# A four-layer graph network on one core: gate columns as products of their own, and a last layer with five whole blocks, paired normalisations and an early overflow count

## The chip, the cores and the metric

The kernel runs on one core of one Trainium2 chip. A core has a matrix engine (TensorE, PE in the profile, with its weight loads as PEld), a vector engine (VectorE, DVE), an activation engine (ScalarE, ACT), a general engine that here mostly issues gathers (GpSimd, POOL), a queue engine (SyncE, SP) and 16 DMA engines. The metric is the device time of one execution in microseconds (us), as the median of several executions. One profiled execution gives the trace that is read below.

## The reference, cut to what matters

There are 2708 nodes with 512 features each. The adjacency matrix is sparse and sorted so that its first rows and columns are the densest. Four layers follow each other, each with a residual and a layer normalisation.

```python
x = layernorm(x + L0(x, adj))          # normalised adjacency @ x @ W.T + b
x = layernorm(x + L1(x, adj))          # (adj + scaled mask) @ x, over its row sums
# layer 2: attention and plain convolution, each with a gate
attn_a = sigmoid(concat([adj @ x, x]) @ Wa.T + ba)
attn_b = sigmoid(concat([adj @ x, x]) @ Wb.T + bb)
h   = x @ W_sa
x_a = softmax_like(adj, h) @ h
x_b = adj @ (x @ W_gcnb) + b_gcnb
x = layernorm(x + sigmoid(attn_a * x_a + attn_b * x_b))
# layer 3
xw = (x > 0) @ sign(weight).T
x = layernorm(x + relu(adj @ xw))
```

## The kernel before

The 2708 nodes make 22 blocks of 128 rows (the last has 20). For every block of rows the kernel finds at its start which columns of the adjacency are not zero, and keeps the columns' numbers (`index`) and their values, packed into tiles of 128 columns (`packed`). Block b has room for `ROOM[b]` such tiles; should one have more, a counter `n_over` is above zero and a dense version of all layers runs afterwards, in an `If` at the end. With these inputs it doesn't run. In a layer, each tile of a block is a gather of 128 rows of features by an indirect DMA, issued by GpSimd, and a matmul.

```python
ROOM = (0, 9, 8, 7, 7, 6, 6, 6, 5, 5, 5, 5, 5, 4, 4, 4, 4, 4, 4, 4, 4, 1)


DIRECT = {1: (0, 1), 2: (0,), 3: (0,), 5: (0,), 8: (0,), 9: (0,),
          13: (0,), 14: (0,), 15: (0,), 16: (0,), 17: (0,)}
...
WHOLE3 = 4
```

The overflow counter is made at the end of the search, as a float:

```python
        nc.tensor.matmul(tot[0:1, :NB], ones, found, start=True, stop=True)
        n_over = const.tile([1, 1], F32, name="s_n_over")
        nc.vector.tensor_tensor(room, tot[0:1, :NB], room, op=ALU.is_gt)
        nc.vector.tensor_reduce(n_over, room, axis=AX.X, op=ALU.add)
```

In layer 2 a block accumulates adj @ x and the attention sums, transposed, in `acc`; they are copied to `pt` and multiplied by the weights. The two columns by which the gates weigh adj @ x lie beside the 512 columns of `W_gcnb`, so that the second half of that product is 258 wide and goes, with the attention's sum, into the PSUM tile `pc`:

```python
        H = D // 2

        def project2(b: int):
            m = rows(b)
            st = state[b]
            acc = st["acc"]
            pt = op.tile([P, KC, 2, P], F32, tag="pt", name=f"pt2_{b}", bufs=1)
            for k in range(0, KC, 2):
                nc.scalar.copy(
                    pt[:, k : k + 2, :, :m],
                    acc[:, k : k + 2, :].rearrange("p k (h i) -> p k h i", h=2)[:, :, :, :m],
                )
            pc = ps_s2.tile([P, KC * P], F32, tag="sm", name=f"pc{b}")
            nc.tensor.matmul(pc[:m, 0:1], st["esum"][:, :m], ones, start=True, stop=True)
            ph = ps_pr.tile([P, D], F32, tag="pr", name=f"ph{b}")
            pg = ps_pr.tile([P, D], F32, tag="pr", name=f"pg{b}")
            for h, ps, w in (
                (0, pg[:m, :H], wg[:, :, :H]), (0, pc[:m, 1 : H + 3], wg[:, :, H:]),
                (1, ph[:m], wsa),
            ):
                for k in range(KC):
                    nc.tensor.matmul(
                        ps, pt[:, k, h, :m], w[:, k, :], start=(k == 0), stop=(k == KC - 1)
                    )
            st.update(pc=pc, ph=ph, pg=pg)

        def finish2(b: int):
            ...
            t = work.tile([P, D], F32, tag="t", name=f"t2_{b}")
            nc.vector.tensor_scalar(t[:m], bg_row[:m], att[:m, 1:2], None, op0=ALU.mult)
            for th, ps in ((t[:m, :H], pg[:m, :H]), (t[:m, H:], pc[:m, 1 : H + 1])):
                nc.vector.scalar_tensor_tensor(
                    th, ps, att[:m, 1:2], th, op0=ALU.mult, op1=ALU.add
                )
            nc.vector.scalar_tensor_tensor(
                t[:m], ph[:m], att[:m, 3:4], t[:m], op0=ALU.mult, op1=ALU.add
            )
```

The last layer splits every adjacency value into a high and a low part, so a tile takes two matmuls (`halves_of`: one copy on ScalarE, one subtraction on VectorE), and widens the features from 16 bits (`widened`). The first `WHOLE3` = 4 blocks take all columns, with no gather: their adjacency comes as a 128 x 512 tile per column block (`whole_tile`), and their four sums stay in PSUM. The others gather. Six whole tiles go ahead, then two after each gathered block:

```python
    with tc.tile_pool(name="s_l3", bufs=13, reuse_waits="tile") as lp, \
            tc.tile_pool(name="s_ps_w", bufs=1, reuse_waits="tile", space=PSUM) as ps_w, \
            tc.tile_pool(name="s_ps_3", bufs=4, reuse_waits="tile", space=PSUM) as ps_3:
...
        def finish3(b: int, ps):
            m = rows(b)
            old = f[b] if b else first[1]
            t = work.tile([P, D], F32, tag="t", name=f"t3_{b}")
            nc.vector.scalar_tensor_tensor(
                t[:m], ps[:m], 0.0, old[:m, :D], op0=ALU.max, op1=ALU.add
            )
            o = work.tile([P, D], F32, tag="xb", name=f"o{b}")
            last = layernorm(o[:m], t, m, f"3_{b}")
            nc.sync.dma_start(out[b * P : b * P + m, :], o[:m])
            return last

        sources3 = {}

        def gather3(b: int):
            sources3[b] = [gathered(lp, D, xw_rows, b, t, F32R) for t in range(ROOM[b])]

        gather3(WHOLE3)


        whole = [ps_w.tile([P, D], F32, tag=f"w{b}", name=f"l3_{b}") for b in range(WHOLE3)]


        def whole_tile(j: int):
            ...
            a = lp.tile([P, W3], F32, tag="aw", name=f"aw{j}", bufs=4)
            nc.sync.dma_start(a[:r], adj_t[j * P : j * P + r, :W3])
            p = halves_of(a[:r], r, W3, f"w{j}")
            for b in range(WHOLE3):
                for h in range(2):
                    nc.tensor.matmul(
                        whole[b], p[:r, h, b * P : (b + 1) * P], g[:r, :],
                        start=(j == 0 and h == 0), stop=(j == NB - 1 and h == 1),
                    )
            if j == NB - 1:
                for b in range(WHOLE3):
                    finish3(b, whole[b])

        AHEAD3 = 6
        for j in range(AHEAD3):
            whole_tile(j)
        j = AHEAD3
        for b in range(WHOLE3, NB):
            ...
            xo = widened(xo, m, f"o{b}")
            if b > WHOLE3:
                gather3(b)
            src = [xw0] * len(direct(b)) + sources3.pop(b)
            ...
            for h in range(2):
                nc.tensor.matmul(
                    ps[:m], dp[:m, h, :m], xo[:m, :], start=(h == 0), stop=False
                )
            ...
                for i in range(n):
                    for h in range(2):
                        nc.tensor.matmul(
                            ps[:m], p[:, h, i * m : (i + 1) * m], src[i0 + i],
                            start=False, stop=(i0 + i == len(src) - 1 and h == 1),
                        )
            last = finish3(b, ps)
            for _ in range(2):
                if j < NB:
                    whole_tile(j)
                    j += 1
        with tc.issue_after(last.ins):
            nc.vector.tensor_copy(over, n_over)
```

`layernorm` there is nine small or wide operations: `bn_stats` and `bn_aggr` on VectorE, a square root on ScalarE with one Newton step on VectorE, and the scaling of the row on VectorE. The outer kernel ends with the test of the counter:

```python
    n_over = nc.values_load(over[0:1, 0:1], min_val=0, max_val=-(-x.shape[0] // P))
    with tc.If(n_over > 0):
        dense_layers(tc, *args)
```

## Time and profile before

| what | value |
|---|---|
| time, median of 3 | 1090.33 us (1087.86 to 1091.51) |
| span of the profiled execution | 1088.5 us |
| PE busy | 956.7 us, 88% |
| DVE busy | 729.7 us, 67% |
| POOL busy | 535.7 us, 49% |
| ACT busy | 404.2 us, 37% |
| bytes moved by DMA | 193.53 MB, mean 178 GB/s |

How it is read: a busy share is an average over stages that have different limits, so it says little by itself. The view of busy time by stage, the waits of one engine, the chain of work that ended last and the groups by line of the kernel say what ends a stage. A matrix multiplication in 32-bit floats appears as two instructions. PEld runs beside PE. A tensor's name in the profile is that of the program with the buffer number left out: `pc`, `pg`, `ph` are products of layer 2, `px` its last product, `pw` and `p` the split tiles, `xg` a gathered tile, `l` a sum of the last layer, `t` and `o` the rows before and after normalisation.

### The profile page before, as it was taken

The numbers are of one execution on the slowest core, as the hardware profiler recorded it, in microseconds if no ns is written. First come the engines' busy times: TensorE is split into PE (matmuls) and PEld (weight loads), VectorE is DVE, ScalarE is ACT, GpSimd is POOL, SyncE is SP. The second block draws the span as 40 slices with busy tenths as digits, with TensorE's granted clock in tenths as the row PEclk, the third lists the DMA queues.
The fourth block names the chain that finished last, engine by engine and source line by source line (L and its number), as shares of the span: only waits on it lengthen the run. The fifth ranks groups of instructions, "written<-read, shape, count | busy, mean of one in ns | idle before, by whom it ended". The sixth has DMA issues, their size and how long they took to land. (4 is left out here: it accounts for less than half of the span.)

```text
span 1088.5 us, 13527 instructions
## 1 busy us (share of the span) xinstructions
PE 956.7 (88%) x4009; PEld 607.7 (56%) x4028; DVE 729.7 (67%) x2578; ACT 404.2 (37%) x869; POOL 535.7 (49%) x545
## 2 busy tenths in 40 slices
PE   2999991899996899998999999999999999789972
PEld 1545440344442345556767777777777777577740
DVE  3998895357774878886576665556666564357865
ACT  4666650010001466785233322322323332165520
POOL 0577777777764777752323223312312221067771
PEclk9999995899996999999999999999999999989995
DMA  9999955778875678872323222322311212199993
GB/s 315 333 385 351 322 173 149 231 237 247 246 247 200 203 220 238 237 211 87 99 63 94 78 64 80 86 69 55 97 53 54 79 45 59 58 312 361 300 261 111
DMA packets 84523, 193.53 MB, mean 178 GB/s; under 512 B 13680, under 2 KB 26968, under 8 KB 84440
## 3 DMA queue, kind: packets, MB, share of 16 engines
q0 software_dynamic: 41056, 113.12, 37.1%
q1 hardware_dynamic: 31692, 64.45, 16.9%
q10 hardware_dynamic: 11692, 15.01, 4.2%
q8 instruction: 34, 0.56, 0.2%
q14 instruction: 49, 0.40, 0.1%
HBM read 155.73 MB, written 25.92 MB: 167 GB/s over the span
## 5 line engine op out<-in xcount | busy, mean ns | idle before, releaser
L1494 POOL DMA_INDIRECT xg<-x_rows,i x107 | 104.0, 972 | 210.6 <-DVE mv L619 59.1
L1336 PE MATMUL acc<-ae,xg 128*128 128x256 f32 x856 | 187.6, 378 | 0.0
L1336 PEld LDWEIGHTS acc<-ae,xg 128*128 128x128 f32 x856 | 162.1, 190 | 22.1 <-ACT ae L1329 0.4
L928 POOL DMA_INDIRECT a<-in_adj_t_dram,row_at x107 | 116.9, 1092 | 65.7 <-DVE mask L782 34.0
L570 POOL DMA_INDIRECT xg<-x_rows,i x107 | 112.0, 1047 | 49.0 <-issue 21.0
L1254 PE MATMUL l<-xg,a 128*128 128x512 f32 x214 | 104.9, 626 | 25.8 <-DMA xg<-y_rows,i 25.8
L570 POOL DMA_INDIRECT xg<-y_rows,i x107 | 104.2, 974 | 32.6 <-issue 17.1
L1400 PE MATMUL l<-xg,inc 128*128 128x512 f32 x214 | 101.1, 609 | 11.9 <-DMA xg<-x_rows,i 10.4
L570 POOL DMA_INDIRECT xg<-xw_rows,i x83 | 83.4, 1005 | 32.6 <-issue 11.9
L958 PE MATMUL y<-s_w,xt 128*128 128x512 f32 (+1 forms) x176 | 84.4, 624 | 0.0
L621 POOL TENSOR_TENSOR rs<-mv,s_neg_half 128x1 f32<-128x1 f32 (+1 forms) x22 | 12.7, 577 | 137.9 <-DVE mv L619 137.6
L1254 PEld LDWEIGHTS l<-xg,a 128*128 128x128 f32 x214 | 39.3, 195 | 73.3 <-issue 57.7
L1537 PE MATMUL ph<-s_wsa,pt 128*128 128x512 f32 (+1 forms) x176 | 79.1, 592 | 0.0
L1325 ACT ACTIVATE ae<-sl,xg 128x128 f32<-128x128 f32 x107 | 40.5, 394 | 103.5 <-DMA xg<-x_rows,i 91.3
L1400 PEld LDWEIGHTS l<-xg,inc 128*128 128x128 f32 x214 | 39.6, 192 | 66.9 <-issue 32.4
L1336 PE MATMUL acc<-ae,f 128*128 128x256 f32 (+1 forms) x272 | 66.5, 389 | 5.9 <-ACT ae L1377 2.9
L1326 DVE SCALAR_TENSOR_TENSOR ae<-ae 128x128 f32<-128x128 f32 (+4 forms) x69 | 29.0, 421 | 63.7 <-ACT ae L1325 63.7
L1336 PEld LDWEIGHTS acc<-ae,f 128*128 128x128 f32 (+1 forms) x272 | 52.2, 194 | 23.1 <-issue 8.9
L615 DVE BATCH_NORM_STATS2 st<-t 128x6 f32<-128x512 f32 (+1 forms) x88 | 60.6, 689 | 1.1
L733 ACT ACTIVATE unused<-arow 128x1408 uint8<-128x1408 f32 (+3 forms) x44 | 58.3, 1325 | 1.1 <-DMA arow<-in_adj_dram 0.3
L1740 PE MATMUL l<-xg,p 128*128 128x512 f32 (+1 forms) x166 | 48.9, 419 | 10.4 <-DMA xg<-xw_rows,i 9.9
L599 ACT ACTIVATE rsqs<-mv 128x1 f32<-128x1 f32 (+1 forms) x66 | 13.3, 202 | 117.7 <-DVE mv L619 113.0
(251 smaller groups left out, 1778.8 us busy)
## 6 DMA issues: line engine op xcount, KB each, us to landing
arow<-in_adj_dram SPq DMA_DIRECT2D x21, 704.0 KB
arow<-in_adj_dram SPq DMA_DIRECT2D x21, 650.0 KB
x_rows<-f SPq DMA_DIRECT2D x21, 258.0 KB
aw<-in_adj_t_dram SPq DMA_DIRECT2D x21, 256.0 KB
out_dram<-o SPq DMA_DIRECT2D x21, 256.0 KB
f<-in_x_dram SPq DMA_DIRECT2D x20, 256.0 KB
y_rows<-yt ACTq DMA_DIRECT2D x20, 256.0 KB
x_rows<-f SPq DMA_DIRECT2D x20, 256.0 KB
```

What stands on the lines that cost most here:

```text
L570: nc.gpsimd.indirect_dma_start(out=t[:, :dst_w], out_offset=None, in_=src[:, :], in_offset=bass.IndirectOffsetOnAxis(ap=index[b][:, i : i ...
L615: nc.vector.bn_stats(st[:m], t[:m])
L733: nc.scalar.activation(unused[:m, : ar.shape[1]], ar, AF.Copy, accum_out=row_sums[:m, b, h : h + 1])
L928: nc.gpsimd.indirect_dma_start(out=packed[b][:, t + len(direct(b)), :], out_offset=None, in_=adj_t, in_offset=bass.IndirectOffsetOnAxis(ap ...
L958: nc.tensor.matmul(ps[:m], xt[:, k, :m], w0[:, k, :], start=(k == 0), stop=(k == KC - 1))
L1254: nc.tensor.matmul(ps[:m], packed[b][:, i, :], moving[:, :D], start=(i == 0), stop=(i == len(src) - 1),)
L1325: nc.scalar.activation(ev[:, i, :], sl, AF.Identity, bias=score)
L1336: nc.tensor.matmul(acc[:, k, :].rearrange("p (h i) -> p h i", h=2)[:, :, :m], src[:r, k * P : (k + 1) * P], ae[:r, :, :m], start=(is_first ...
L1400: nc.tensor.matmul(ps[:m], inc[:, i, :m], src[i0 + i][:, :D], start=(i0 + i == 0), stop=(i0 + i == len(src) - 1),)
L1494: nc.gpsimd.indirect_dma_start(out=g, out_offset=None, in_=x2_rows[:, :], in_offset=bass.IndirectOffsetOnAxis(ap=index[b][:, t : t + 1], a ...
L1537: nc.tensor.matmul(ps, pt[:, k, h, :m], w[:, k, :], start=(k == 0), stop=(k == KC - 1))
L1740: nc.tensor.matmul(ps[:m], p[:, h, i * m : (i + 1) * m], src[i0 + i], start=False, stop=(i0 + i == len(src) - 1 and h == 1),)
```

## The change

It has four parts. In layer 2 the gates' two columns get a weight tile of their own (`wab`) and four narrow products per block, and the product with `W_gcnb` is done in one piece of 512 columns, with one VectorE operation after it in place of two. In the last layer five blocks take all columns in place of four; the block of 20 rows is gathered first; whole tiles are handed out by the number of gathers done (one for every three) in place of two a block, with five ahead; and there are 11 gather buffers in place of 13. Normalisations of the last layer are done for two blocks together: their small operations are shared, and ScalarE writes the rows; a whole block is the partner of a gathered one near the end. Finally the overflow counter is copied to its integer already in the search, and not after the last row. The purpose is to take gathers from GpSimd, to spread the end's work on VectorE, and to let the engines test the counter without waiting for the last row.

```diff
--- before.py
+++ after.py
@@ -37,7 +37,11 @@
 GROUPS = (
     (1,), (2, 3), (4, 5, 6), (7, 8, 9), (10, 11, 12), (13, 14, 15), (16, 17, 18), (19, 20), (21,),
 )
-WHOLE3 = 4
+
+
+WHOLE3 = 5
+AHEAD3 = 5
+FETCHES3 = 3
 
 
 def over_partitions(row: bass.AP, n: int):
@@ -1135,9 +1139,10 @@
             nc.vector.memset(room[:, b : b + 1], float(P * ROOM[b]))
         tot = ps_s.tile([P, D], F32, tag="find", name="tot", bufs=2)
         nc.tensor.matmul(tot[0:1, :NB], ones, found, start=True, stop=True)
-        n_over = const.tile([1, 1], F32, name="s_n_over")
+        n_over = pre.tile([1, 1], F32, name="s_n_over")
         nc.vector.tensor_tensor(room, tot[0:1, :NB], room, op=ALU.is_gt)
         nc.vector.tensor_reduce(n_over, room, axis=AX.X, op=ALU.add)
+        nc.vector.tensor_copy(over, n_over)
 
     work = ctx.enter_context(tc.tile_pool(name="s_work", bufs=2, side="right", reuse_waits="tile"))
 
@@ -1284,8 +1289,9 @@
     nc.scalar.dma_start(own_row[:, 1, :], over_partitions(wb[0, D:], D))
     bg_row = wp2.tile([P, D], F32, name="s_bg_row")
     nc.scalar.dma_start(bg_row, over_partitions(b_gcnb, D))
-    wg = wp2.tile([P, KC, D + 2], F32, name="s_wg")
-    nc.scalar.dma_start(wg[:, :, :D], w_gcnb.rearrange("(k p) o -> p k o", p=P))
+    wg = wp2.tile([P, KC, D], F32, name="s_wg")
+    nc.scalar.dma_start(wg, w_gcnb.rearrange("(k p) o -> p k o", p=P))
+    wab = wp2.tile([P, 2, KC], F32, name="s_wab")
     l2_ps = ctx.enter_context(ExitStack())
     ps_acc = l2_ps.enter_context(
         tc.tile_pool(name="s_ps_acc", bufs=2, side="right", reuse_waits="tile", space=PSUM)
@@ -1358,10 +1364,7 @@
     with tc.tile_pool(name="s_l1", bufs=8, reuse_waits="tile") as lp:
         pv = ps_mm.tile([P, D], F32, tag="mm", name="pv2")
         nc.tensor.transpose(pv[:, : 2 * KC], vrows, ident[: 2 * KC, : 2 * KC])
-        nc.vector.tensor_copy(
-            wg[:, :, D:].rearrange("p k t -> p t k"),
-            pv[:, : 2 * KC].rearrange("p (t k) -> p t k", t=2),
-        )
+        nc.vector.tensor_copy(wab.rearrange("p t k -> p (t k)"), pv[:, : 2 * KC])
 
         def grow2(j: int, n: int):
 
@@ -1513,8 +1516,6 @@
                     b, st["src"][i0 + i], ae[:, i], P, c == 0 and i == 0, last and i == n - 1
                 )
 
-        H = D // 2
-
         def project2(b: int):
             m = rows(b)
             st = state[b]
@@ -1527,15 +1528,16 @@
                 )
             pc = ps_s2.tile([P, KC * P], F32, tag="sm", name=f"pc{b}")
             nc.tensor.matmul(pc[:m, 0:1], st["esum"][:, :m], ones, start=True, stop=True)
+            for k in range(KC):
+                nc.tensor.matmul(
+                    pc[:m, 1:3], pt[:, k, 0, :m], wab[:, :, k], start=(k == 0), stop=(k == KC - 1)
+                )
             ph = ps_pr.tile([P, D], F32, tag="pr", name=f"ph{b}")
             pg = ps_pr.tile([P, D], F32, tag="pr", name=f"pg{b}")
-            for h, ps, w in (
-                (0, pg[:m, :H], wg[:, :, :H]), (0, pc[:m, 1 : H + 3], wg[:, :, H:]),
-                (1, ph[:m], wsa),
-            ):
+            for h, ps, w in ((0, pg, wg), (1, ph, wsa)):
                 for k in range(KC):
                     nc.tensor.matmul(
-                        ps, pt[:, k, h, :m], w[:, k, :], start=(k == 0), stop=(k == KC - 1)
+                        ps[:m], pt[:, k, h, :m], w[:, k, :], start=(k == 0), stop=(k == KC - 1)
                     )
             st.update(pc=pc, ph=ph, pg=pg)
 
@@ -1547,7 +1549,7 @@
             att = small.tile([P, 4], F32, tag="att", name=f"att{b}")
             nc.vector.tensor_scalar(att[:m, 2:3], pc[:m, 0:1], SUM_EPS, None, op0=ALU.add)
             nc.vector.reciprocal(att[:m, 2:3], att[:m, 2:3])
-            nc.vector.tensor_tensor(att[:m, 0:2], pc[:m, H + 1 : H + 3], own[:m, 1:3], op=ALU.add)
+            nc.vector.tensor_tensor(att[:m, 0:2], pc[:m, 1:3], own[:m, 1:3], op=ALU.add)
 
 
             nc.scalar.activation(att[:m, 0:2], att[:m, 0:2], AF.Tanh, scale=0.5)
@@ -1557,10 +1559,9 @@
             )
             t = work.tile([P, D], F32, tag="t", name=f"t2_{b}")
             nc.vector.tensor_scalar(t[:m], bg_row[:m], att[:m, 1:2], None, op0=ALU.mult)
-            for th, ps in ((t[:m, :H], pg[:m, :H]), (t[:m, H:], pc[:m, 1 : H + 1])):
-                nc.vector.scalar_tensor_tensor(
-                    th, ps, att[:m, 1:2], th, op0=ALU.mult, op1=ALU.add
-                )
+            nc.vector.scalar_tensor_tensor(
+                t[:m], pg[:m], att[:m, 1:2], t[:m], op0=ALU.mult, op1=ALU.add
+            )
             nc.vector.scalar_tensor_tensor(
                 t[:m], ph[:m], att[:m, 3:4], t[:m], op0=ALU.mult, op1=ALU.add
             )
@@ -1633,9 +1634,9 @@
 
 
 
-    with tc.tile_pool(name="s_l3", bufs=13, reuse_waits="tile") as lp, \
+    with tc.tile_pool(name="s_l3", bufs=11, reuse_waits="tile") as lp, \
             tc.tile_pool(name="s_ps_w", bufs=1, reuse_waits="tile", space=PSUM) as ps_w, \
-            tc.tile_pool(name="s_ps_3", bufs=4, reuse_waits="tile", space=PSUM) as ps_3:
+            tc.tile_pool(name="s_ps_3", bufs=3, reuse_waits="tile", space=PSUM) as ps_3:
         W3 = WHOLE3 * P
         CH3 = 4
         PW = max(CH3 * P, W3)
@@ -1660,24 +1661,48 @@
                 nc.scalar.copy(g[:r], t[:r])
             return g
 
-        def finish3(b: int, ps):
+        moments = []
+
+        def finish3(b: int, ps, more: bool):
+
             m = rows(b)
             old = f[b] if b else first[1]
-            t = work.tile([P, D], F32, tag="t", name=f"t3_{b}")
+            k = len(moments)
+            t = work.tile([P, D], F32, tag=("t", "xb")[k], name=f"t3_{b}")
             nc.vector.scalar_tensor_tensor(
                 t[:m], ps[:m], 0.0, old[:m, :D], op0=ALU.max, op1=ALU.add
             )
-            o = work.tile([P, D], F32, tag="xb", name=f"o{b}")
-            last = layernorm(o[:m], t, m, f"3_{b}")
-            nc.sync.dma_start(out[b * P : b * P + m, :], o[:m])
-            return last
+            st = small.tile([P, 6], F32, tag="st", name=f"st_3_{b}")
+            nc.vector.bn_stats(st[:m], t[:m])
+            mv = moments[0][2] if k else small.tile([P, 2, 2], F32, tag="mv3", name=f"mv_3_{b}")
+            nc.vector.bn_aggr(mv[:m, k, :], st[:m])
+            moments.append((b, t, mv))
+            if more:
+                return
+            n = len(moments)
+            rs = small.tile([P, 2, 2], F32, tag="rs3", name=f"rs_3_{b}")
+            mean, v = mv[:m, :n, 0], mv[:m, :n, 1]
+            nc.vector.tensor_scalar(v, v, LN_EPS, None, op0=ALU.add)
+            rsqrt_of(rs[:m, 0, :n], v, m, n, f"3_{b}")
+            nc.vector.scalar_tensor_tensor(
+                rs[:m, 1, :n], mean, -1.0, rs[:m, 0, :n], op0=ALU.mult, op1=ALU.mult
+            )
+            for k, (b, t, _) in enumerate(moments):
+                nc.scalar.activation(
+                    t[:m], t[:m], AF.Identity, bias=rs[:m, 1, k : k + 1],
+                    scale=rs[:m, 0, k : k + 1],
+                )
+                nc.sync.dma_start(out[b * P : b * P + m, :], t[:m])
+            moments.clear()
 
         sources3 = {}
 
         def gather3(b: int):
             sources3[b] = [gathered(lp, D, xw_rows, b, t, F32R) for t in range(ROOM[b])]
 
-        gather3(WHOLE3)
+        order3 = [NB - 1, *range(WHOLE3, NB - 1)]
+        gather3(order3[0])
+        gather3(order3[1])
 
 
         whole = [ps_w.tile([P, D], F32, tag=f"w{b}", name=f"l3_{b}") for b in range(WHOLE3)]
@@ -1699,21 +1724,18 @@
                         whole[b], p[:r, h, b * P : (b + 1) * P], g[:r, :],
                         start=(j == 0 and h == 0), stop=(j == NB - 1 and h == 1),
                     )
-            if j == NB - 1:
-                for b in range(WHOLE3):
-                    finish3(b, whole[b])
-
-        AHEAD3 = 6
-        for j in range(AHEAD3):
+        j = 0
+        while j < AHEAD3:
             whole_tile(j)
-        j = AHEAD3
-        for b in range(WHOLE3, NB):
+            j += 1
+        due = 0
+        for at, b in enumerate(order3):
             m = rows(b)
             xo = lp.tile([P, D], F16, tag="xo", name=f"xo{b}", bufs=3)
             nc.sync.dma_start(xo[:m], xw_rows[b * P : b * P + m, :])
             xo = widened(xo, m, f"o{b}")
-            if b > WHOLE3:
-                gather3(b)
+            if at + 1 < len(order3) and at:
+                gather3(order3[at + 1])
             src = [xw0] * len(direct(b)) + sources3.pop(b)
             ps = ps_3.tile([P, D], F32, tag="mm", name=f"l3_{b}")
 
@@ -1741,13 +1763,17 @@
                             ps[:m], p[:, h, i * m : (i + 1) * m], src[i0 + i],
                             start=False, stop=(i0 + i == len(src) - 1 and h == 1),
                         )
-            last = finish3(b, ps)
-            for _ in range(2):
-                if j < NB:
-                    whole_tile(j)
-                    j += 1
-        with tc.issue_after(last.ins):
-            nc.vector.tensor_copy(over, n_over)
+            pending = bool(moments)
+            finish3(b, ps, not pending and b not in (order3[0], order3[-1]))
+            if j == NB and whole and len(moments) == 1:
+                finish3(WHOLE3 - len(whole), whole.pop(0), False)
+            due += ROOM[b]
+            while j < NB and due >= FETCHES3:
+                whole_tile(j)
+                j += 1
+                due -= FETCHES3
+        while whole:
+            finish3(WHOLE3 - len(whole), whole.pop(0), len(whole) % 2 == 1)
```

## The prediction, made before the change was run

> **What bounds the kernel now.** I read the page's slices first: TensorE (PE) is busy at 0.9 or more for most of the span, with its clock granted in full, and the last slices sag. Busy time by stage then gives two stages that the change touches. The second stretch below is the first half of the last layer, the third and fourth its thin end (columns: window, length, busy us and count of PE, PEld, DVE, ACT, POOL, granted clock, DMA share, GB/s):
>
> ```profile
> 500.00:955.00 455.00, 432.51 (x1870) 327.34 (x1888) 269.69 (x815) 139.71 (x362) 116.70 (x129) 0.99 0.26 72
> 955.00:1026.00 71.00, 69.28 (x291) 55.43 (x292) 52.39 (x131) 38.85 (x81) 53.76 (x53) 0.97 1.15 335
> 1026.00:1059.00 33.00, 25.04 (x85) 15.13 (x84) 24.08 (x87) 11.52 (x31) 25.06 (x27) 0.95 0.98 278
> 1059.00:1088.50 29.50, 7.79 (x22) 2.93 (x20) 16.45 (x66) 1.53 (x8) 4.57 (x5) 0.61 0.39 120
> ```
>
> Layer 2 (500 to 955) is TensorE's: 432.5 of 455 us. What PE waits for there, from 560 to 955, is little, and no gather is among it:
>
> ```profile
> PE pc L1537 <- ACT pt L1524: 9.8, 16, 0.9
> PE tb L1582 <- DVE bx L1574: 5.1, 1, 5.1
> PE px L1587 <- ACT xt L1584: 1.0, 2, 0.7
> ```
>
> So every us of work added to TensorE in layer 2 is a us of span. The last layer is different. The chain that ended last shows whole tiles (L1698) and block products (L1740) without a break at first, then gathers, then a VectorE tail:
>
> ```profile
> 1015.17 3.63 PE l L1698 x16
> 1019.25 2.27 PE l L1740 x10
> ...
> 1052.44 4.20 DMA xg<-xw_rows,i
> 1056.69 1.22 PE l L1740 x2
> ...
> 1072.32 0.68 DVE t L1667
> 1073.13 0.60 DVE st L615
> ```
>
> The group of the gathers says why: 83 of them, 0.94 us each, from 956.4 to 1063.8, a start every (1063.85 - 956.38)/82 = 1.31 us. GpSimd issues them without a pause in 108 us while PE needs only 394 matmuls x 0.227 us (3.63 us for 16) = 89 us, and 1.8 us more because the first eight run cold (628 ns each, starting 0.45 us apart). The last matmul ends near 1069.8; four whole blocks finished at once have left VectorE behind, so the last row is issued at 1075.85, 119.8 us after the layer's first matmul (956.08). Then 12.65 us pass with no work. The lines of the closing code show it:
>
> ```profile
> L1783 POOLq TENSOR_LOAD <-over x1: 492/492/492, 1075.9 to 1075.9; - x1
> L1784 POOLq COMPARE_BRANCH  x1: 53/53/53, 1076.5 to 1076.5; - x1
> L1824 POOLq DRAIN  x3: 50/107/7173, 1080.5 to 1088.2; - x3
> SPq L1824 <- PEq L1824: 6.3, 2, 5.7
> ```
>
> All engines load the overflow count only after VectorE copied it, at 1075.9; GpSimd branches, starts its drain at 1080.5 and holds everybody for 7.17 us. SyncE is ready at 1082.1 and waits 5.7 us.
>
> **What the Trainium skill says.** "TensorE: Matmul & The Clock Gate", section LDWEIGHTS: a load costs its columns divided by 1.2 in ns, 107 for 128 columns. The trace agrees where the moving operand is short: eight f32 matmuls of 40 columns in layer 2 follow each other every 0.111 us, each with its own load. The same page, section on the HAM clock gate, has a cold array for about 3.4 us; here the first eight matmuls of the layer take 3.58 us. "DMA: Bandwidth & Descriptors", section "Where 436 GB/s comes from", has an HBM limit near 358 GB/s per core; this trace moves 356 to 380 in the windows from 960 to 1010, so the last layer's transfers are near a limit as well. "Runtime: NRT & Kernel Launch", section on instruction fetch, has a taken branch fetch its target; here an engine does nothing for 3.3 to 3.9 us after the branch.
>
> **The change, part by part.** *Layer 2, the gate columns.* Before, the two columns rode on the second half of the W_gcnb product (258 instead of 256 columns). An f32 matmul is two instructions, so a block had 8 of 256 columns at 0.2155 and 8 of 258 at 0.2175 us: 3.46 us. After, 8 of 512 columns at 0.4295 = 3.44 us (the spacing of the same shape in `ph`), plus 4 matmuls of 2 columns = 8 instructions that cost their weight loads, 8 x 0.111 = 0.89 us. Net +0.86 us for each of 21 blocks, and about 0.6 for the block of 20 rows: **+18.7 us**, all on the path. VectorE gets one 512-column operation (0.75 as for `ph`) in place of two of 0.48, and the gates' numbers come 3.4 us earlier; neither sets PE's pace, so I count nothing for them.
>
> *Last layer, five whole blocks.* Block 4's seven gathers go: 76 remain. PE gets 22 x 5 x 2 = 220 whole-tile matmuls, 76 x 2 + 8 x 2 block products and 17 x 2 for the blocks' own rows: 422 x 0.227 = 95.8, with the cold start 97.6 us. GpSimd: 75 x 1.31 + 0.3 = 98.6 us to the last gather's start, and 2.8 us to its landing (1063.85 to 1066.66 in the trace) = 101.4. The two are now almost equal, which is what the interleaving is for: a whole tile (10 matmuls, 2.27 us) for every three gathers (3.9 us). Up to block 14, 52 gathers and 17 tiles after the first five, PE has 356 matmuls = 80.8 + 1.8 us; the eleven gather buffers let GpSimd be 11 gathers ahead, so 13 are left, 13 x 1.31 + 2.8 = 19.8 us. That sums to 102.4 us for the last matmul, without any slip. DMA has about the bytes of before: 76 x 262 KB of gathers, 22 x 459 KB of tiles, 2.2 MB of own rows and 5.5 MB out = 37.7 MB, of which 1.8 MB come early; at 365 GB/s 98 us. Three limits within 5 us will not mesh without loss: I add 1.5 us.
>
> *Normalisation in pairs.* VectorE per block before: 0.68 + 0.69 + 0.18 + 0.15 + 0.15 + 0.21 + 0.14 + 0.15 + 0.54 = 2.9 us. A pair after: twice (0.68 + 0.69 + 0.18), once about 1.04 of small ones: 2.07 per block. Some 17 us leave VectorE, and ScalarE gets 22 x 0.63, in a layer where it is busy 38.85 of 71 us. On the path only the end counts: the backlog of 6.0 us between the last matmul and the last issue becomes one block's chain: 0.68 + 0.69 + 0.18 + 0.15, the root 0.20 and two handovers of 0.1, 0.15 + 0.21 + 0.14 + 0.15 + 0.15, 0.63 on ScalarE: 3.5, with a little still queued 4.1 us. First matmul to last issue: 102.4 + 1.5 + 4.1 = 108 instead of 119.8: **-11.8 us**.
>
> *Overflow count.* GpSimd can load it after its last gather, at 99.5 us of the layer; 4.6 us to its drain and 7.2 in it (the durations above) make 111.3. SyncE reaches its own end 6.3 us after the last issue (1075.85 to 1082.12), at 114.3. The drain is hidden: **-5.6 us**.
>
> Sum: 1090.3 + 18.7 - 11.8 - 5.6 = 1091.6, say 1092 us.
>
> **Rivals.** (a) The small matmuls are nearly free because PE idles for `pt` anyway (9.8 us in 16 waits, which stand exactly there). Against it: they need `pt` too, so they come after the wait. If half were hidden: 1083. (b) The reverse: before, the two wide `pc` matmuls (0.87 us) covered the 0.6 us in which ScalarE copies `xt`; two narrow ones (0.44) do not, and PE would wait some 0.2 us a block more: 1096. (c) In the last layer VectorE becomes the bound: blocks 15 to 19 each finish with a whole block, 4.1 us and about 1.2 us of splitting and casts, against 5.2 us of gathers for four tiles. VectorE works in order, and a split of the next block queued behind a pair would stall PE. For it: it was 0.8 to 0.9 busy from 1010 to 1030. That would eat 5 to 6 us: 1097. (d) The meshing is perfect and the tail short: 103 us for the layer, 1086. (e) GpSimd's drain doesn't begin before the others arrive, so the end stays at 12.65 us: 1097.
>
> **Range and chances.** Layer 2's term is sure to about +-3 us, the last layer's to +-7, the end's to +-3; they are independent, some +-8 in all, and I widen for what a new order of instructions may do: 1080 to 1105. Two per cent are 22 us. Faster than 1068 needs a last layer under 95 us, less than PE's own work, or layer 2 for nothing: 0.03. Slower than 1112 needs the last layer to gain nothing and waits on top: 0.05.
>
> **What would show it.** Layer 2, by its lines: 176 extra matmul instructions 0.11 us apart, and the layer's end (the last `px`, 951.2 now) near 970; if it stays below 960, (a). In the last layer: 76 gathers, PE without a gap to about 82 us after its first tile, last issue 108 us after it; PE idle for VectorE's split would be (c), a landing wait in the first 80 us a DMA limit. At the end: GpSimd's load of the count well before the last output, 7 us instead of 12.65 after the last issue. The prediction is wrong if layer 2 does not grow by 16 to 22 us, or if the last layer's gain is outside 5 to 18.

## Result and profile after

| | before | after |
|---|---|---|
| time, median of 4 | 1090.72 us (1087.86 to 1091.51) | 1102.86 us (1098.49 to 1103.61) |
| ratio, 95% interval | | 1.0108 [1.0075, 1.0140] |
| span of the profiled execution | 1088.5 us | 1100.6 us |
| layer 2: first attention sum (matmul `pc<-s_ones,esum`) to first matmul of the last layer | 452.8 us | 474.1 us |
| last layer: first to last matmul | 113.7 us | 105.8 us |
| last matmul to issue of the last row | 6.0 us | 11.4 us |
| issue of the last row to the end | 12.66 us | 5.96 us |

The changed kernel is slower by 12.1 us. The rows below the span are read from the starts and ends of the instructions named, and they carry the difference: +21.3 in layer 2, -2.6 in the last layer (first matmul to last row 119.8 and 117.2 us), -6.7 at the end. With 0.1 from the layers ahead that is +12.1, the difference of the two spans.

Busy time by stage of the changed kernel, with the columns as in the prediction (PE, PEld, DVE, ACT, POOL, granted clock, DMA share, GB/s). The last three windows are the last layer while whole tiles run, its thin end, and what comes after the last matmul:

```profile
500.00:955.00 455.00, 440.70 (x1823) 308.93 (x1840) 260.15 (x773) 135.09 (x346) 118.34 (x128) 0.99 0.25 68
533.50:540.90 7.40, 7.40 (x14) 3.60 (x15) 2.72 (x13) 0.20 (x1) 1.90 (x2) 0.54 0.13 36
977.40:1060.00 82.60, 82.57 (x355) 67.19 (x356) 55.85 (x134) 48.93 (x94) 62.84 (x62) 0.98 1.18 339
1060.00:1083.30 23.30, 18.93 (x69) 13.06 (x67) 18.69 (x66) 10.09 (x23) 13.60 (x15) 0.92 0.87 248
1083.30:1100.60 17.30, 0.00 (x0) 0.00 (x0) 6.46 (x28) 5.54 (x10) 0.00 (x0) 0.50 0.31 111
```

Layer 2 is still TensorE's. In the last layer PE works 82.57 of the first 82.60 us, as the interleaving was meant to make it. The last line is the one to stop at: 17.3 us pass after the last matmul, 11.4 of them before the last row is issued, and VectorE is busy for only 6.46 us and ScalarE for 5.54. So in that stretch somebody waits. The second line, a stretch with a lower clock, is taken up under the experiments.

Layer 2, first by what PE waits for from 560 to 975, then by the new line of narrow products:

```profile
PE pc L1532 <- ACT pt L1525: 11.2, 17, 1.2
PE tb L1583 <- DVE bx L1575: 5.1, 1, 5.1
PE px L1588 <- ACT xt L1585: 1.0, 2, 0.7
```

```profile
L1532 PE MATMUL pc<-s_wab,pt x176: 164/251/353, 504.1 to 958.8; 128*128 128x2 f32 x168, 128*20 128x2 f32 x8
```

The waits are those of before (9.8, 5.1 and 1.0), and the 176 matmul instructions come on top: the idle time in front of `pc` was not filled by the narrow products, because they need `pt` as well.

The closing code, first where the engines load the counter, then what GpSimd does at the end:

```profile
L1809 SPq TENSOR_LOAD <-over x1: 469/469/469, 164.9 to 164.9; - x1
L1809 POOLq TENSOR_LOAD <-over x1: 783/783/783, 1073.0 to 1073.0; - x1
...
L1809 ACTq TENSOR_LOAD <-over x1: 486/486/486, 1092.6 to 1092.6; - x1
```

```profile
L1850 POOLq DRAIN  x3: 50/107/7295, 1078.5 to 1100.0; - x3
```

Each engine now loads the counter when it gets there itself. SyncE has it at 164.9. GpSimd starts its drain at 1078.5, before the last matmul, and its 7.3 us are over at 1085.8, when the last three rows have not even begun. Before, the drain began at 1080.5 with everything else done.

Now the thin end on VectorE, in order of time (start, duration, instruction, and in brackets the idle time before it and its releaser):

```profile
1079.98 0.69 DVE L1672 SCALAR_TENSOR_TENSOR t<-l,f 128x512 f32<-128x512 f32 x1 [1.47 <-DMA out_dram<-t]
1080.59 0.15 DVE L608 RECIPROCAL rsqs<-rsqs 128x2 f32<-128x2 f32 x1
...
1086.69 0.69 DVE L1672 SCALAR_TENSOR_TENSOR t<-l,f 128x512 f32<-128x512 f32 x1 [2.05 <-PEq L1810]
```

And on ScalarE, which writes the rows:

```profile
1083.36 2.93 ACT L1691 ACTIVATE t<-t,rs 128x512 f32<-128x512 f32 x4
...
1092.39 2.22 ACT L1691 ACTIVATE t<-t,rs 128x512 f32<-128x512 f32 x3 [1.20 <-DVE rs L1687]
```

VectorE stands still for a transfer of finished rows. The new code makes the sum in a buffer `t`, ScalarE normalises it there in place, and the output transfer reads the same buffer. So `t` is held from the first operation to the landing of the output, and there are two buffers of each of its two tags, that is two pairs. The row that starts at 1086.69 takes over the buffer of the row begun at 1074.93: that one's output was issued at 1084.20, and the semaphore of that transfer arrives at 1086.57. The profile prints "PEq" as the releaser there, because the instruction waits for more than one semaphore; the one that came last is the transfer's. The wait at 1079.98 is of the same kind, for an output issued at 1075.78. With the two before it (1.31 at 1068.81, 0.32 at 1076.67) VectorE waits 5.15 us for outputs.

The second line shows how it feeds on itself: the reciprocal at 1080.59 belongs to the pair before and has its input long before, but stands behind the blocked `t` in VectorE's order. Without it ScalarE cannot write that pair's rows, so their output leaves late, so the next `t` is blocked again.

### The profile page after: what moved, and what is told of

Its sections match the earlier page's. It is cut to its first block, busy times and chain, and to the rows that moved or that the text cites. A ratio compares the mean times of both kernels' runs of the same rounds, so it can differ in the third digit from the quotient of the medians.

```text
span 1100.6 us, 13499 instructions
## 1 busy us (share of the span) xinstructions
PE 978.0 (89%) x4037; PEld 602.8 (55%) x4056; DVE 716.1 (65%) x2502; ACT 419.8 (38%) x878; POOL 530.9 (48%) x538
## 5 line engine op out<-in xcount | busy, mean ns | idle before, releaser
L1497 POOL DMA_INDIRECT xg<-x_rows,i x107 | 105.8, 989 | 216.7 <-DVE mv L623 63.9
L1259 PE MATMUL l<-xg,a 128*128 128x512 f32 x214 | 103.9, 620 | 27.6 <-DMA xg<-y_rows,i 27.5
L574 POOL DMA_INDIRECT xg<-xw_rows,i x76 | 76.4, 1006 | 31.8 <-issue 12.8
L1539 PE MATMUL pg<-s_wg,pt 128*128 128x512 f32 (+1 forms) x176 | 84.4, 622 | 0.0
L1539 PEld LDWEIGHTS ph<-s_wsa,pt 128*128 128x128 f32 (+1 forms) x176 | 32.7, 186 | 42.6 <-issue 42.2
L603 ACT ACTIVATE rsqs<-mv 128x1 f32<-128x1 f32 (+2 forms) x56 | 11.2, 202 | 114.5 <-DVE mv L623 102.9
```

What stands on the lines that cost most here:

```text
L574: nc.gpsimd.indirect_dma_start(out=t[:, :dst_w], out_offset=None, in_=src[:, :], in_offset=bass.IndirectOffsetOnAxis(ap=index[b][:, i : i ...
L1259: nc.tensor.matmul(ps[:m], packed[b][:, i, :], moving[:, :D], start=(i == 0), stop=(i == len(src) - 1),)
L1497: nc.gpsimd.indirect_dma_start(out=g, out_offset=None, in_=x2_rows[:, :], in_offset=bass.IndirectOffsetOnAxis(ap=index[b][:, t : t + 1], a ...
L1539: nc.tensor.matmul(ps[:m], pt[:, k, h, :m], w[:, k, :], start=(k == 0), stop=(k == KC - 1))
```

## Experiments

They ran in three groups of four, on other chips than the pair above. The kernel before took 1196.3, 1193.8 and 1186.5 us beside the three groups: the layers before layer 2 take 67 to 96 us more there (its first attention sum comes at 570 to 599 us instead of 503), and the gathers of the last layer start every 1.46 to 1.51 us instead of 1.31. Layer 2 itself takes about the same time (the old one 453.0 to 457.1 us, 452.8 in the first pair). So each time is compared with the kernel before beside it, and stages with stages of these groups alone. The variants were made from the two kernels, so their lines differ by a few numbers.

The first theory is that layer 2 grew by the weight loads of the narrow products, that the early counter works as intended, and that the last layer lost its gain to the row buffers. Rivals: the narrow products cost less alone; VectorE's work, not its buffers, is the bound at the end; and the pairing is at fault, since it makes two rows wait for each other.

### One part of the change at a time: l2_only, count_only, l3_only

l2_only is the kernel before with the change's layer 2 and nothing else:

```diff
+            for k in range(KC):
+                nc.tensor.matmul(pc[:m, 1:3], pt[:, k, 0, :m], wab[:, :, k], ...)
...
-                (0, pg[:m, :H], wg[:, :, :H]), (0, pc[:m, 1 : H + 3], wg[:, :, H:]),
-                (1, ph[:m], wsa),
+            for h, ps, w in ((0, pg, wg), (1, ph, wsa)):
```

> The kernel before with only layer 2's part of the change: the gates' two columns as four narrow products per block, the rest untouched. Theory 1 (the narrow products cost their weight loads on a busy TensorE, as the trace of the change has it: first matmul of the last layer 21.3 us later): 1090.7 + 21 = 1112, between 1109 and 1114. Rival (the narrow products fall into TensorE's waits, and the last layer is what lost): below 1100.

Measured: ratio 1.0150 [1.0102, 1.0199], median 1211.03 us. Layer 2 takes 472.3 us against 453.0 in count_only, the kernel with the old layer 2 in the same group: +19.4 us. The last layer (135.7 us to the last row) and the end (12.47) are as in the kernels with the old ones. The step stands, and rival (a) falls.

count_only is the kernel before with the counter copied early:

```diff
-        n_over = const.tile([1, 1], F32, name="s_n_over")
+        n_over = pre.tile([1, 1], F32, name="s_n_over")
...
+        nc.vector.tensor_copy(over, n_over)
...
-        with tc.issue_after(last.ins):
-            nc.vector.tensor_copy(over, n_over)
```

> The kernel before with only the overflow count copied in the search. Theory 1 (GpSimd's drain of 7.2 us then runs beside the last rows): 5.6 to 6.7 us off, 1084 to 1085.5, and 6 to 7 us between the last output's issue and the end. Rival (the drain begins only when all have arrived): 1090 to 1091, and 12.6 us at the end.

Measured: 0.9952 [0.9928, 0.9975], which is -5.7 us of 1196.3. From the last row to the end it takes 5.39 us, although the drain's record is 10.13 us long in this profile (it begins at 1158.9, before the last gather at 1160.90): it lies beside the last rows. Rival (e) falls.

l3_only is the changed kernel with the old layer 2 (the hunk of l2_only in reverse), so the new last layer and the early counter together:

> The changed kernel with layer 2 as before (gate columns beside the others, 258 wide), so only the last layer and the early count differ from the kernel before. Theory 1: 1102.9 - 21 = 1082, between 1079 and 1085; the last layer from its first matmul to its last output 117 us and the end 6 us. Rival (layer 2 is nearly free): 1095 or more.

Measured: 0.9893 [0.9840, 0.9947], median 1184.0 us. Of the 12.8 us that this is of 1196.3, the counter alone brings 5.7. The last layer takes 129.5 us to its last row against 135.6 in count_only, -6.1, where the prediction had -11.8; 11.7 us lie between last matmul and last row. Layer 2 took 457.1 us here with the code that took 453.0 in count_only. Of that 2.9 us lie between its first blocks (31.1 instead of 28.2 us): PE waits 2.31 us for ScalarE's `ae` there instead of 1.08, and then the clock stands at 0.50 from 607.4 to 610.8, so that the next sixteen products take 5.41 instead of 3.72 us.

### Row buffers taken out of the way: rows_in_place

The row is made in the tile of the old features, which nobody reads after it. Each block has its own, so no row waits for another's output:

```diff
-            t = work.tile([P, D], F32, tag=("t", "xb")[k], name=f"t3_{b}")
+            t = old[:, :D]
```

> The changed kernel, but a row of the last layer is written over the old features of its block, which nothing reads afterwards, so it needs none of the four row buffers. Theory 1 (the rows' buffers are held until the output has landed, VectorE in its order waits for them, and with it TensorE's split and the last three rows): no wait of VectorE on an output; last output 5 to 7 us after the last matmul instead of 11.4, last matmul 2 us earlier; 1095, between 1093 and 1098. Rival (VectorE's own work for pairs is too much at the end): within 2 us of 1102.9.

Measured: 0.9971 [0.9950, 0.9992] over 20 executions. The same instructions on the same engines, and the tail after the last matmul is 5.1 us. Busy time after the last matmul of rows_in_place:

```profile
1180.30:1191.50 11.20, 0.02 (x1) 0.00 (x0) 2.97 (x16) 3.94 (x6) 0.00 (x0) 0.63 0.34 123
```

The unaltered changed kernel was run again in the second group (after_again, no edit):

> The changed kernel unaltered, as the yardstick for the three runs beside it. Both theories: 1.1 per cent (12 us) above the kernel before where the layers' transfers are as quick as in the first profile; some 11.4 us from the last matmul to the last output.

Measured: 1.0047 [1.0023, 1.0070]; a disadvantage of 5.6 us instead of 12.1. Its busy time after the last matmul, and the line of VectorE's waits in the last layer that has the outputs:

```profile
1176.10:1196.90 20.80, 0.02 (x1) 0.00 (x0) 9.46 (x41) 5.58 (x10) 0.00 (x0) 0.57 0.26 93
```

```profile
DVE t L1672 <- DMA out_dram<-t: 4.0, 2, 2.6
```

VectorE has 41 operations still to do after the last matmul, against 16 with the rows in place; the tail is 14.9 us against 5.1, and the last layer 132.0 against 124.2: -7.8 us by one line that changes no work. On rows_in_place's own chip the new last layer with its buffers is that of l3_only: 129.5 us, a tail of 11.7, so -5.3 us for the same line. Not all of the shorter tail is gain: the last matmul, expected 2 us earlier, came 119.1 us after the first instead of 117.1 and 117.8, and VectorE had more done by then. Among the waits of VectorE in rows_in_place's last layer there is none for an output; the longest at that line is for a sum:

```profile
DVE f L1672 <- PE l L1751: 4.3, 1, 4.3
```

This is the run that separates the theories. Rival (c) has VectorE's work as the bound; the work is unchanged, and the tail is gone. The two ran on different chips, each with its own kernel before; the intervals of the two ratios do not overlap, and lie some 9 us apart, where theory 1 had 8.

Why the changed kernel loses less here than in the first pair (5.6 against 12.1 us) stays open. Against count_only and l2_only its stages give +20.4 in layer 2, -3.6 in the last layer and -6.6 at the end, +10.2 in sum; the rest would lie ahead of layer 2, where single runs on these chips differ by more than that (the kernel before from 1183 to 1204 us in this group).

### The narrow products doubled: narrow_twice

The changed kernel does them twice, the first time into columns that nobody reads:

```diff
-            for k in range(KC):
-                nc.tensor.matmul(pc[:m, 1:3], pt[:, k, 0, :m], wab[:, :, k], ...)
+            for at in (3, 1):
+                for k in range(KC):
+                    nc.tensor.matmul(pc[:m, at : at + 2], pt[:, k, 0, :m], wab[:, :, k], ...)
```

> The changed kernel with the four narrow products of every block of layer 2 done twice, the first time into two columns that nobody reads. Theory 1 (each narrow instruction costs its weight load of 0.11 us on a busy TensorE): 22 x 8 x 0.11 = 19.4 us more than the changed kernel. Rival (only their place behind the copy, or the loss of what covered it, cost the time): under 6 us more.

Measured: 1.0238 [1.0166, 1.0311]. Its line of narrow products:

```profile
L1533 PE MATMUL pc<-s_wab,pt x352: 164/251/354, 595.0 to 1068.8; 128*128 128x2 f32 x168, 128*20 128x2 f32 x8
```

The count is doubled (352; the split by shape behind it lists only 176). Layer 2 takes 493.3 us against 473.4 in after_again: +20.0 us for another 176 instructions, 0.114 us each. With 0, 176 and 352 of them the layer takes 453.0 (count_only), 472.3 (l2_only) and 493.3 us, all but a straight line.

The first pair had +21.3 us in layer 2. Part of the surplus is the second line of the windows shown first: from 533.5 to 540.9 the clock was granted at 0.54, and the wide products there took twice their time. PE at that place:

```profile
536.12 4.95 PE L1539 MATMUL pg<-s_wg,pt 128*128 128x512 f32 x6
```

Eight such products take 3.6 us elsewhere. The eight `pg` there, from 533.57 to 540.91 with four narrow ones between them, took 7.3 us: some 3.4 us lost. The stretch follows 16 products of 40 columns and the narrow ones. after_again, the same kernel on another chip, has it at the same eight products:

```profile
615.90:623.30 7.40, 7.40 (x15) 3.58 (x15) 2.70 (x12) 0.20 (x1) 1.89 (x2) 0.54 0.13 36
```

narrow_twice has it in the same block (627.8 to 634.6, clock 0.50). rows_in_place, alone and l2_only, which do the narrow products too, don't have it there (alone and l2_only have one of 3.4 us later, at 635.8 and 799.5), and no kernel with the old layer 2 has it there; so whether the narrow products bring it on is not known. rows_in_place has the new layer 2 with the clock in full, and is of one chip with count_only: 471.2 against 453.0 us. The narrow products alone thus cost 18.3 us, and the clock about 3 more in the first pair.

### Pairs or single rows: alone

Every row is normalised for itself, in the changed kernel with its four row buffers used in turn, and each of the five whole blocks follows one gathered block near the end:

```diff
-            finish3(b, ps, not pending and b not in (order3[0], order3[-1]))
-            if j == NB and whole and len(moments) == 1:
+            finish3(b, ps, False)
+            if j == NB and whole and at >= len(order3) - 6 and at < len(order3) - 1:
...
-            t = work.tile([P, D], F32, tag=("t", "xb")[k], name=f"t3_{b}")
+            t = work.tile([P, D], F32, tag=("t", "xb")[one[0] % 2], name=f"t3_{b}")
```

> The changed kernel with every row of the last layer normalised by itself, still written by ScalarE, the four row buffers used in turn; blocks 15 to 19 each still finish together with a whole block. Theory 1 (buffers, not the amount of VectorE's work, make the end long): a row is held shorter, so the end shortens in spite of 11 more sets of small operations: 8 to 10 us from last matmul to last output instead of 11.4, 1 to 3 us below the changed kernel. Rival (VectorE's work sets the end): 11 x 1 us more work, the end longer than 11.4 us and the kernel 3 us or more slower than the changed one.

Measured: 1.0029 [1.0005, 1.0053], and the interval overlaps that of after_again. The tail is 11.9 us; one wait of 1.5 us for an output is left. The run does not say whether the pairs or the buffers held up the end; it was too small a step, and it moves the order of the whole blocks as well.

### A version that beats both: best, best_again, best_whole4, best_alone, old_layer_rows

best has the old layer 2, the new last layer with the rows in place, and the early counter:

```diff
-            for k in range(KC):
-                nc.tensor.matmul(pc[:m, 1:3], pt[:, k, 0, :m], wab[:, :, k], ...)
...
-            t = work.tile([P, D], F32, tag=("t", "xb")[k], name=f"t3_{b}")
+            t = old[:, :D]
```

> Layer 2 as before, the changed last layer and the early count, and the rows of the last layer written over the old features. Theory 1 (three separate terms: narrow products +19, row buffers +6, both gone here): 25 us below the changed kernel, 12 to 15 us below the kernel before, ratio to before 0.985 to 0.990. Rival (the last layer is limited by its transfers, so that free rows only move the wait): no faster than the changed last layer with its row buffers, 18 to 21 us below the changed kernel.

Measured: 0.9826 [0.9764, 0.9889], by the medians 25.5 us below after_again, as theory 1 has it, and 20.7 below the kernel before, more than it has. Busy time after its last matmul:

```profile
1157.70:1169.50 11.80, 0.01 (x1) 0.00 (x0) 2.95 (x16) 3.95 (x6) 0.00 (x0) 0.70 0.32 118
```

That is the end of rows_in_place, without the narrow products. The same kernel in the third group, no edit:

> Once more layer 2 as before, the changed last layer, the early count and the rows written over the old features, as the yardstick for the three beside it. Both theories: 1.7 per cent below the kernel before, ratio 0.976 to 0.989; 5 to 6 us from last matmul to last output.

Measured: 0.9839 [0.9814, 0.9865], -19.1 us of 1186.5. The last layer takes 122.2 and 125.5 us in the two, against 129.5 in l3_only, from which they differ by the line of the row alone. A stage read from one profile is thus sure to some 3 us; but the three paired layers with rows in place (122.2 to 125.5) and the three with the buffers (129.3 in narrow_twice to 132.0) don't overlap.

best_whole4 gives one whole block back to the gathers:

```diff
-WHOLE3 = 5
+WHOLE3 = 4
```

> The same with four whole blocks, all other rules of the last layer kept. Theory 1 (a gather of GpSimd paces the last layer, 1.33 to 1.5 us each): seven gathers more and nothing else on the path: 7 to 11 us more than with five whole blocks. Rival (TensorE and the transfers pace it as much as GpSimd): 4 us more or less.

Measured: 0.9884 [0.9853, 0.9916], 6.2 us above best_again by the medians. It gathers 83 times and its last matmul comes 126.1 us after the first instead of 120.7, its last row at 130.4 instead of 125.5. The fifth whole block is worth 5 to 6 us, between the two expectations.

best_alone is best with single rows, by the first part of the edit of alone:

> The same with five whole blocks, but every row normalised by itself, still written by ScalarE over the old features. Theory 1 (once rows need no buffer, the share of small operations that pairs save lies beside other work except at the very end): within 3 us of the pairs, 5 to 8 us from last matmul to last output. Rival (pairs matter: 11 sets of small operations of about 1 us): 5 us or more slower.

Measured: 0.9808 [0.9770, 0.9846]; the interval overlaps that of best_again. Its last layer takes 127.7 us against 125.5, and its lower median comes from the layers before layer 2, which ended 10 us earlier in its profile and are the same code. With the rows out of the way, pairing brings nothing that these runs can show.

old_layer_rows is count_only with the row of the old last layer made in place:

```diff
-            t = work.tile([P, D], F32, tag="t", name=f"t3_{b}")
+            t = o = old[:, :D]
...
-            o = work.tile([P, D], F32, tag="xb", name=f"o{b}")
```

> The kernel before, its four whole blocks finished at once and its own normalisation on VectorE, with two edits: the early count and rows written over the old features. Theory 1 (its tail of 6 us and more is VectorE's work on a backlog, and its row buffers hold only until a row is scaled): 0 to 3 us below the kernel with the early count alone, ratio to the kernel before 0.992 to 0.996. Rival (row buffers were the hidden limit of the old last layer as well): 6 us or more below it, ratio under 0.990.

Measured: 0.9927 [0.9900, 0.9953], overlapping with count_only (0.9952). Its tail is short (4.6 us), but the last matmul came later, at 134.1 us instead of 125.4, so that the last row is no earlier (138.8 against 135.6). Going by the total time, row buffers were not what limited the old layer. The gathers start every 1.51 us here and every 1.47 in count_only, which is 3.7 us over 82 of them; why, and what makes the rest of the 8.7, is open.

## Why the prediction was right or wrong

| term | predicted | first pair | with one cause alone |
|---|---|---|---|
| layer 2 | +18.7 | +21.3 | +18.3 at full clock (rows_in_place), +19.4 (l2_only), +20.0 for as many again |
| last layer, to its last row | -11.8 | -2.6 | -6.1 with the row buffers (l3_only); -11.4, -13.4, -10.1 with the rows in place |
| end | -5.6 | -6.7 | -5.7 in the time, -7.1 at the end itself (count_only) |
| sum | +1.3 | +12.1 | |

The time, 1102.86 us, lies inside the range of 1080 to 1105, but that is the width of the range: in its middle stood +1.3 us, and +12.1 came. By the prediction's own test it was wrong: the last layer's gain was to be between 5 and 18 us, and was 2.6.

**Layer 2: right.** "8 x 0.111 = 0.89 us" a block, all on the path, is what the runs measured: 18.3 us at full clock, where +18.7 was predicted. That the first pair had 21.3 is the stretch with the lower clock, which the prediction didn't foresee. Rival (a) fell by the wait in front of `pc`, which is as long as before. Rival (b), a wait for `xt`, fell too: 1.0 us in 2 waits, before and after, since `px` runs between the two halves of the narrow products.

**The counter: right.** The drain was hidden as the working had it, and the end is 5.96 us instead of the 7 expected.

**The last layer up to its last matmul: nearly right.** Predicted 103.9, measured 105.8. PE was without a gap to 82.6 us, as predicted. The last gather started at 99.9 instead of 98.6 (the group has a start every 1.329 us, not 1.31), and the last pair of products began 5.2 us after that start and not 2.8. The 2.8 were a wrong reading: the products at 1066.66 of the kernel before used the gather begun at 1062.61, 4.0 us earlier, and those of the gather begun at 1063.85 came at 1068.78, after 4.9 us. One wait of 2.50 us for VectorE's `dp`, at 1071.46, looks like rival (c), but ScalarE had handed on both `dp` by 1067.6, and VectorE came to the first only at 1071.01, after the `t` that had waited 1.31 us for an output at 1068.81 and what had piled up behind it:

```profile
1071.46 0.73 PE L1751 MATMUL l<-wo,dp 128*128 128x512 f32 x2 [2.50 <-DVE dp L1746]
```

What the two smaller pools of the diff do (11 gather buffers for 13, and 3 tiles for the sums `l` for 4) was not run by itself.

**The tail: wrong, and this is the step that failed.** "On the path only the end counts: the backlog of 6.0 us between the last matmul and the last issue becomes one block's chain: ... with a little still queued 4.1 us." It was 11.4 us. The working counted the durations of VectorE and ScalarE, and asked for no buffer's life. Before, VectorE read the sum from `t` and wrote the row into `o`, so that only `o` was held for the transfer, and from its last operation on. After, one buffer goes through sum, normalisation and transfer: the row begun at 1074.93 held its own until 1086.57, 11.6 us: 9.3 to the issue of its output, with the wait for its partner and VectorE's stops in it, and 2.4 to the landing. The diff shows it in two lines, `t[:m], t[:m]` in ScalarE's call and `out[...], t[:m]` after it. The next three rows held theirs for 10.5, 8.2 and 8.7 us. Four buffers held for 9.8 us on average let a row begin every 2.4 us (an estimate from these numbers), more than the 2.07 us of VectorE's work that the prediction had for one. That the buffers are the cause is shown by rows_in_place, which changes nothing else, and by best against l3_only.

With the rows in place, the tail was 4.4 to 5.5 us in five kernels with the new layer, close to the 4.1 predicted, and with five whole blocks in pairs the last layer gained 10 to 13 us against count_only, around the 11.8 (on chips where both layers take longer; 11.4 on count_only's own). So the arithmetic of the work was sound, and the tail makes up 7.3 of the 9.2 us by which the term was off. Rival (d), a short tail at 1086, and (e), a late drain, did not happen. (c) had the right engine standing in the way, but took its work for the cause; it was its waiting.

The Trainium skill could have warned of it: "DMA: Bandwidth & Descriptors", section "Anatomy of one DMA", gives a transfer a fixed cost of about 2.0 us, most of it the confirmation of the last write, before its semaphore moves. The section speaks of transfers issued by GpSimd; the output rows here are SyncE's, and the trace has 2.4 us (1084.20 to 1086.57) and up to 4.6 (1076.48 to 1081.05) from issue to the last step of the semaphore.

## What to carry to other kernels

When a change moves an operation to another engine, write down for each buffer who writes it first and who reads it last, and put the transfer's landing into its life; two buffers that were enough for a short life may be too few for a long one, although every engine has less to do. A narrow product is not free: with a weight load of its own it costs the load, so a few columns are better carried on a wide product that loads the same weights. What only decides what happens after the end should be computed as early as its inputs allow.

## What the runs showed of the hardware

- GpSimd's closing drain took 6.6 to 7.3 us (7.69 in alone and 10.13 in count_only, where its record begins while the last gathers still run), and it runs beside the other engines' work: the time from the last row to the end fell from 12.66 to 5.96 us when GpSimd could branch early.
- A 32-bit product of 2 columns in four steps takes 8 matmul instructions and, with their loads, 0.8 to 0.9 us a block (18.3 to 20.0 us for 22), a quarter of the time of the product with 512 columns (3.44 us).
- The clock fell to 0.54 for 7.4 us while PE was busy for all of them, at the same products in both profiles of the changed kernel and in the same block of narrow_twice. "TensorE: Matmul & The Clock Gate", section "Why this matters for your kernels", asks for no idle gaps of more than some 3 us between bursts; the trace shows no gap there (7.50 of 7.50 us busy before it at a clock of 1.00). Its cause is open.
- The same program's early layers differed by some 80 us between chips, while layer 2, which TensorE bounds, took 452.8 us on the first and 453.0 to 457.1 on the others.
